# A graph layer's edge loop: weights, edge attributes and index offsets read from SBUF instead of PSUM, one-hot tiles built per twelve tiles

## The chip, the core and the metric

The kernel runs on one core of a Trainium2 chip. The metric is the device time of one execution in microseconds. The engines are TensorE (PE in the profile), VectorE (DVE), ScalarE (ACT), GpSimd (POOL) and SyncE (SP, which here only starts transfers).

## The reference

A message-passing layer with 12,500 nodes of 160 features (64 scalars, and 32 vectors of 3) and 400,000 edges sorted by destination, all in float32:

```python
h = relu(layernorm(x))
s0, s1 = x0 @ W_sc0 * a, einsum(x1, W_sc1) * a          # self part; x0, x1: scalars, vectors of h
y0, y1 = x0 @ W_l1_0 * a, einsum(x1, W_l1_1) * a        # what is sent; a = node_vec1
w = silu(e16 @ fc_W1) @ fc_W2                             # per edge, 192 weights: a (64), b (64), c (32), d (32)
ys0, ys1 = y0[src], y1[src]                             # gather
e0, e1 = e4[:, :1], e4[:, 1:]                           # 4 numbers per edge
mid0 = concat(w_a * ys0 * e0, w_d * sum_c(ys1 * e1))    # 96 scalars
mid1 = concat((w_b * ys0) x e1, (w_c * e0) x ys1)       # 96 vectors of 3
z0, z1 = zeros.at[dst].add(mid0), zeros.at[dst].add(mid1)
out = x + C_S * s + C_X * (z0 @ W_l2_0, einsum(z1, W_l2_1)) * a
```

Constant factors (fan-in, the number of neighbours) are left out above. In the program `e16` is the (400000, 16) array from which the 192 weights come, and `e4` the (400000, 4) array of `e0` and `e1`.

## The kernel before

**Node stage.** 98 tiles of 128 nodes, two at a time: VectorE makes mean, variance and relu(x - mean), PE turns and multiplies, ScalarE scales rows out of PSUM, one DMA per eight tiles stores the sent rows in the DRAM tensor `y_d`, and GpSimd adds the self part to x in `acc`, which stays in SBUF for the whole kernel.

**Index work.** `relate` (L119 to L159) turns the destination of each edge into `drel`, its distance from the first node of its window; a window is three tiles of 128 edges (`WT`), whose destinations must lie within 32 nodes (`WN`). Edges that lie farther go through a fallback at the end (from L572), a loop that runs zero or one time by a flag. The work runs on VectorE over all 3125 tiles at once, with operands in SBUF.

**Edge loop.** 3125 tiles of 128 edges are handled in blocks of four tiles (`GT`), 782 blocks; three blocks are a group of twelve tiles (`TG`). For a block b:

- `load(b)`: GpSimd gathers 128 rows of `y_d` by the indices in `src_sb` for each tile, one indirect DMA per tile (L398), into a `yg` buffer for the block. There are ten such buffers and the calls run eight blocks ahead (`AHEAD`).
- `hidden_pair`: PE (L407) and ScalarE (L412, silu) make the hidden layer for two blocks each.
- `weigh(b)`: PE writes the 192 weights per edge to the PSUM tile `pw` (L429), of which there are two. `scale` (L349, ScalarE) multiplies the first 96 by `e0` in place, and L350 copies `e1` and `drel` (four numbers per tile) into `pw` behind the weights. These come from `ev`, which `e4_load` and `e4_join` make once per 96 tiles (a DMA to `raw`, then copies of `raw` and `drel` by ScalarE, L445 and L446).
- `select(b)`: VectorE compares `iota` with the `drel` in `pw` (L460), which gives a one-hot tile over 32 nodes, and multiplies it by the three numbers of `e1` in `pw` (L462), into a quarter of `sel`.
- `products(b)`, through `multiply`: VectorE makes `tmp` from `yg` and `e1` (L355), sums it over the three components (L357), and writes the products of weights and rows into `pr` (L358, L359, L360, L362).
- `sums(b)`: PE multiplies `sel` and `pr` (L480), adding over a window's three tiles in PSUM; ScalarE copies a finished window out (L485, L487).
- `turn`, `linear`, `add`, `accumulate`: one group behind, one stage per block (`accumulate` in the third): transposes, the output weights, a 0/1 matrix `place` (L508) that puts the windows' rows onto two node tiles, and two additions into `acc` by VectorE (L525).

The order on PE, ScalarE and VectorE is the order of the calls, written out by hand (`manual_schedule`); GpSimd and SP run their own instructions in program order as semaphores allow. For block b the loop calls `load(b + 8)`, `weigh(b + 2)`, a stage of the group before, `select(b + 1)`, `products(b + 1)`, perhaps `accumulate`, `sums(b)`, and on every fourth block `hidden_pair`. At the end `acc` goes to the output in twelve large DMAs.

Of the kernel before, what the change touches and what calls it, by code (L numbers as in the profile page):

```python
# [10 lines left out]
F32 = mybir.dt.float32  # L11
I32 = mybir.dt.int32
AF = mybir.ActivationFunctionType
ALU = mybir.AluOpType
# [4 lines left out]
P = 128  # L19
M0 = 64  # L20
M1 = 32
# [3 lines left out]
NW = 2 * M0 + 2 * M1  # L25
PC = 256
ZC = 384
GT = 4
BT = 32
WN = 32  # L30
WT = 3
GW = 4
TG = WT * GW
EG = 8
# [8 lines left out]
def kernel(  # L43
# [19 lines left out]
    nc = tc.nc  # L63
    N = x.shape[0]
    NT = attr.shape[1]
    TP = src.shape[1]
    T = n_edges // P
    assert n_edges % P == 0 and TP % BT == 0 and NT == (N + P - 1) // P and NT >= 2
    NWIN = (T + WT - 1) // WT
    NG = (NWIN + GW - 1) // GW  # L70
# [11 lines left out]
    iota = const.tile([P, 2 * P], F32, name="iota")  # L82
# [14 lines left out]
    drel = const.tile([P, TP], F32, name="drel")  # L97
# [135 lines left out]
    with (  # L233
# [83 lines left out]
        with tc.manual_schedule(engines=engines):  # L317
# [8 lines left out]
            for q in range(len(steps) + 4):  # L326
                if q <= last and steps[q][2] == 0:
                    g = steps[q][0] + LEAD * GN
# [14 lines left out]
    before.close()  # L343


    def scale(pw, ev, n):

        for k in range(n):
            nc.scalar.activation(pw[:, k, 0:96], pw[:, k, 0:96], AF.Copy, scale=ev[:, k, 0:1])  # L349
        nc.scalar.activation(pw[:, :n, NW:NW + 4], ev[:, :n, 1:5], AF.Copy)  # L350

    def multiply(pr, tmp, wt, yg, n):

        y1 = yg[:, :n, M0:].rearrange("p t (c u) -> p t c u", c=3)
        nc.vector.tensor_tensor(tmp[:, :n, 0:3, :], y1, wt[:, :n, NW:NW + 3].unsqueeze(3).to_broadcast([P, n, 3, M1]),  # L355
                                ALU.mult)
        nc.vector.tensor_reduce(tmp[:, :n, 3, :], tmp[:, :n, 0:3, :].rearrange("p t c u -> p t u c"), AX.X, ALU.add)  # L357
        nc.vector.tensor_mul(pr[:, :n, 192:PC], wt[:, :n, 96:160], yg[:, :n, 0:M0])  # L358
        nc.vector.tensor_mul(pr[:, :n, 0:M0], wt[:, :n, 0:M0], yg[:, :n, 0:M0])  # L359
        nc.vector.tensor_mul(pr[:, :n, 96:192].rearrange("p t (c u) -> p t c u", c=3),  # L360
                             wt[:, :n, M0:96].unsqueeze(2).to_broadcast([P, n, 3, M1]), y1)
        nc.vector.tensor_mul(pr[:, :n, M0:96], wt[:, :n, 160:NW], tmp[:, :n, 3, :])  # L362

    with (
        tc.tile_pool(name="selp", bufs=3) as selp,
        tc.tile_pool(name="prod", bufs=3) as prod,
        tc.tile_pool(name="ld", bufs=2) as ld,
        tc.tile_pool(name="ev", bufs=2) as evp,
        tc.tile_pool(name="yg", bufs=10) as ygp,
        tc.tile_pool(name="hid", bufs=4) as hid,  # L370
        tc.tile_pool(name="post", bufs=2) as post,
# [4 lines left out]
        blocks, ev4, hids, rows, wts, sels, z_ps, z_sb, zT, o_sb, prs, sums_ps = ({} for _ in range(12))  # L376

        def tiles_of(b):
            return list(range(b * GT, min((b + 1) * GT, T)))
# [41 lines left out]
        def weigh(b):  # L421
            hT = hids[b // 2]
            pw = p_w.tile([P, GT, 256], F32, name="pw")
            n = len(tiles_of(b))
            for k in (0, 2, 1, 3):
                if k < n:
                    r = slice(FC_H * (k // 2), FC_H * (k // 2 + 1))
                    o = P * (b % 2 * 2 + k % 2)
                    nc.tensor.matmul(pw[:, k, 0:NW], hT[r, o:o + P], w2[r, :], start=True, stop=True)  # L429
            scale(pw, e4_of(b), n)  # L430
            wts[b] = pw

        def e4_load(q):

            if q * EG < NG and q not in ev4:
                lo, hi = q * EG * TG, min((q + 1) * EG * TG, TP)
                raw = ld.tile([P, EG * TG, 4], F32, name="raw")
                nc.sync.dma_start(raw[:, :hi - lo, :].rearrange("p t c -> p (t c)"), e4[:, lo * 4:hi * 4])
                ev = evp.tile([P, EG * TG, 5], F32, name="ev")
                ev4[q] = ev, raw, lo, hi - lo  # L440

        def e4_join(q):
            if q in ev4:
                ev, raw, lo, n = ev4[q]
                nc.scalar.activation(ev[:, :n, 0:4], raw[:, :n, :], AF.Copy)  # L445
                nc.scalar.activation(ev[:, :n, 4:5], drel[:, lo:lo + n].unsqueeze(2), AF.Copy)  # L446

        def e4_of(b):
            g, k = divmod(b, TG // GT)
            o = g % EG * TG + k * GT  # L450
            return ev4[g // EG][0][:, o:o + GT, :]

        def select(b):

            g, k = divmod(b, TG // GT)
            if k == 0:
                sels[g] = selp.tile([P, TG, 4, WN], F32, name="sel")
            n, wt = len(tiles_of(b)), wts[b]
            sel = sels[g][:, k * GT:k * GT + n, :, :]
            nc.vector.tensor_tensor(sel[:, :, 3, :], iota[:, 0:WN].unsqueeze(1).to_broadcast([P, n, WN]),  # L460
                                    wt[:, :n, NW + 3:NW + 4].to_broadcast([P, n, WN]), ALU.is_equal)
            nc.vector.tensor_tensor(sel[:, :, 0:3, :], sel[:, :, 3:4, :].to_broadcast([P, n, 3, WN]),  # L462
                                    wt[:, :n, NW:NW + 3].unsqueeze(3).to_broadcast([P, n, 3, WN]), ALU.mult)

        def products(b):
            wt, yg = wts.pop(b), rows.pop(b)
            pr = prod.tile([P, GT, PC], F32, name="pr")
            tmp = prod.tile([P, GT, 4, M1], F32, name="tmp")
            multiply(pr, tmp, wt, yg, len(tiles_of(b)))
            prs[b] = pr  # L470

        def sums(b):
# [46 lines left out]
        def accumulate(g):  # L519
            ps = sums_ps.pop(g)  # L520
            i = nc.values_load(tile_i[0:1, g:g + 1], engines=[mybir.EngineType.DVE], min_val=0, max_val=NT - 2,
                               skip_runtime_bounds_check_because="clamped to NT - 2 on the chip, and not negative")
            for h in range(2):
                to = acc[:, ds(i + h, 1), :]
                nc.vector.scalar_tensor_tensor(to, ps[:, h:h + 1, :], a_sb[:, ds(i + h, 1)], to,  # L525
                                               op0=ALU.mult, op1=ALU.add)
# [3 lines left out]
        K = TG // GT  # L530
        order = tc.manual_schedule(engines={mybir.EngineType.PE, mybir.EngineType.Activation, mybir.EngineType.DVE})
        with order:
            for b in range(min(AHEAD, NB)):
                load(b)
            e4_load(0)
            e4_join(0)
            hidden_pair(0)
            weigh(0)
            if NB > 1:
                weigh(1)  # L540
            select(0)
            products(0)
            for b in range(NB):
                g, k = divmod(b, K)
                if b + AHEAD < NB:
                    load(b + AHEAD)
                q, r = divmod(b, EG * K)
                if r == 0:
                    e4_load(q + 1)
                if r == EG * K - 4:  # L550
                    e4_join(q + 1)
                if b + 2 < NB:
                    weigh(b + 2)
                if g:
                    (turn, linear, add)[k](g - 1)
                if b + 1 < NB:
                    select(b + 1)
                    products(b + 1)
                if g and k == K - 1:
                    accumulate(g - 1)  # L560
                sums(b)
                if b % 4 == 0 and b + 4 < NB:
                    hidden_pair((b + 4) // 2)
            for h in ([NG - 2] if NG > 1 else []) + [NG - 1]:
                for k, stage in enumerate((turn, linear, add, accumulate)):
                    if h == NG - 1 or min(k, K - 1) > (NB - 1) % K:
                        stage(h)
# [4 lines left out]
    with (  # L572
# [10 lines left out]
        n = nc.values_load(far_i[0:1, 0:1], min_val=0, max_val=1)  # L583
        with tc.For_i(0, n, 1) as _:
            with tc.For_i(0, ZR, P) as r:
                nc.sync.dma_start(z_d[ds(r, P), :], zero)
            with tc.For_i(0, TP // GT, 1) as g:
                xe = fp.tile([FC_IN, 512], F32, name="f_xe")
                nc.sync.dma_start(xe, e16[ds(g * FC_IN, FC_IN), :])
                er = fp.tile([P, GT, 4], F32, name="f_er")  # L590
                nc.sync.dma_start(er.rearrange("p t c -> p (t c)"), e4[:, ds(g * (GT * 4), GT * 4)])
                ev = fp.tile([P, GT, 5], F32, name="f_ev")
                nc.vector.memset(ev, 0.0)
                si = fp.tile([P, GT], I32, name="f_si")
                nc.sync.dma_start(si, src[:, ds(g * GT, GT)])
                di = fp.tile([P, GT], I32, name="f_di")
# [2 lines left out]
                nc.vector.tensor_copy(df, di)  # L599
                out_of = fp.tile([P, GT], F32, name="f_out")  # L600
                nc.vector.tensor_scalar(out_of, drel[:, ds(g * GT, GT)], float(WN), None, ALU.is_ge)
                nc.vector.tensor_mul(ev[:, :, 0:4], er, out_of.unsqueeze(2).to_broadcast([P, GT, 4]))
                yg = fp.tile([P, GT, D], F32, name="f_yg")
                for k in range(GT):
                    nc.gpsimd.indirect_dma_start(
# [6 lines left out]
                pw = fpw.tile([P, GT, 256], F32, name="f_pw")  # L612
# [1 line left out]
                    nc.tensor.matmul(pw[:, k, 0:NW], hT[:, P * k:P * (k + 1)], w2[0:FC_H, :],  # L614
                                     start=True, stop=True)
                tmp = fp.tile([P, GT, 4, M1], F32, name="f_tmp")
                scale(pw, ev, GT)
                pr = fp.tile([P, GT, PC], F32, name="f_pr")
                multiply(pr, tmp, pw, yg, GT)
                for k in range(GT):  # L620
                    pd = fpp.tile([P, P], F32, name="f_pd")
                    nc.tensor.transpose(pd, df[:, k:k + 1].to_broadcast([P, P]), ident)
                    sel = fp.tile([P, P], F32, name="f_sel")
# [83 lines left out]
```

## Time and profile before

| what | value |
|---|---|
| median of 3 runs | 4176.25 us (4176.24 to 4178.38) |
| the profiled execution | 4178.38 us, its span 4176.5 us |
| POOL busy | 3003.1 us (72%), of which gathers L398 2962.3 us, 3125 of 948 ns |
| PE busy | 3326.4 us (80%), L480 1592.0, L429 758.8 |
| DVE busy | 2885.1 us (69%), six lines of `multiply` 2187, L460 and L462 649 |
| ACT busy | 2641.8 us (63%), L349 985.4, L487 667.5 |
| DMA | 319.85 MB, 77 GB/s over the span |
| gathers | first starts at 219.8 us, last at 4132.8 us |

A share of busy time is over the whole span. A group's row gives an instruction's line, engine, operation, tiles and count, then its busy time, the mean duration of one in ns, and the time that the engine was idle just before it with what ended most of that. Matmuls are pipelined, so a busy PE isn't one at its peak. In rows of the timeline the first two numbers are start and duration in microseconds from the span's start. The names `pw` and `wt` mean one tile in the kernel before: functions that take `wt` are given the PSUM tile `pw`.

### The profile page before, as it was taken

How to read it: one execution, taken by the hardware profiler on the slowest of the kernel's cores; microseconds unless marked ns; L12 is line 12 of the kernel's file. 1: busy time of each engine (PE TensorE's matmuls, PEld its weight loads, DVE VectorE, ACT ScalarE, POOL GpSimd, SP SyncE). 2: the span in 40 equal slices, each digit the busy share in tenths (PEclk: the TensorE clock that was granted, in tenths of full speed). 3: DMA queues.
4: the chain of work that ended last, by engine and by line, in shares of the span. 5: the costliest groups of instructions: out<-in, count | busy, mean ns of one | idle time of the engine just before them, and what ended most of it. 6: DMA issues, size and time to landing. Idle time of an engine off the chain costs nothing.

```text
span 4176.5 us, 61508 instructions
## 1 busy us (share of the span) xinstructions
PE 3326.4 (80%) x17265; PEld 2401.9 (58%) x17265; DVE 2885.1 (69%) x7403; ACT 2641.8 (63%) x9266; POOL 3003.1 (72%) x3150
## 2 busy tenths in 40 slices
PE   8968788877788887788777878777877877778885
PEld 5645555555556555555555555555655555555554
DVE  5477776777777777777777777777777777777774
ACT  3356666666666666666666666666666666666664
POOL 1177777777777777777777777777777777777774
PEclk9999999999999999999999999999999999999998
DMA  4222222222222222222222222222222222222224
GB/s 122 59 78 76 74 76 77 73 76 71 76 76 74 76 76 74 74 74 76 76 73 76 73 76 74 74 76 74 76 76 73 76 74 74 76 74 75 74 72 117
DMA packets 233168, 319.85 MB, mean 77 GB/s; under 512 B 65754, under 2 KB 182566, under 8 KB 232566
## 3 DMA queue, kind: packets, MB, share of 16 engines
q0 software_dynamic: 150000, 256.20, 23.0%
q1 hardware_dynamic: 63412, 47.69, 3.9%
q10 hardware_dynamic: 19410, 11.99, 1.0%
q8 instruction: 139, 2.28, 0.2%
q14 instruction: 207, 1.70, 0.1%
HBM read 299.62 MB, written 16.00 MB: 76 GB/s over the span
## 4 chain that ended last, share of the span: by engine, by line
DVE 24%; DMA 23%; POOL 22%; issue 20%; PE 9%; DVEq 1%; ACT 1%; POOLq 0%
DMA yg<-y_d,src_sb 23%; POOL yg L398 22%; DVE tmp L357 5%; DVE tmp L355 5%; DVE pr L360 3%; DVE pr L359 3%; PE po L299 2%; DVE sel L462 2%; DVE acc L525 2%; DVE pr L362 2%; PE po L298 2%; PE pz L480 1%; DVE sel L460 1%; DVE pr L358 1%; PE pw L429 1%
## 5 line engine op out<-in xcount | busy, mean ns | idle before, releaser
L398 POOL DMA_INDIRECT yg<-y_d,src_sb x3125 | 2962.3, 948 | 953.3 <-issue 736.1
L480 PE MATMUL pz<-pr,sel 128*128 128x256 f32 x6250 | 1592.0, 401 | 0.0
L349 ACT ACTIVATE pw<-pw,ev 128x96 f32<-128x96 f32 x3125 | 985.4, 315 | 938.3 <-PE pw L429 844.4
L429 PE MATMUL pw<-w,hT 64*128 64x192 f32 x6250 | 758.8, 363 | 714.3 <-DVE pr L362 708.1
L480 PEld LDWEIGHTS pz<-pr,sel 128*128 128x128 f32 x6250 | 1228.8, 205 | 151.2 <-issue 0.9
L429 PEld LDWEIGHTS pw<-w,hT 64*128 64x128 f32 x6250 | 515.2, 194 | 1107.6 <-DVE pr L362 956.7
L355 DVE TENSOR_TENSOR tmp<-yg,pw 128x384 f32<-128x384 f32 x782 | 432.7, 553 | 1041.2 <-DMA yg<-y_d,src_sb 1040.3
L487 ACT ACTIVATE zs<-pz 32x64 f32<-32x64 f32 x3126 | 667.5, 214 | 41.4
L357 DVE TENSOR_REDUCE tmp<-tmp 128x128 f32<-128x384 f32 x782 | 463.5, 593 | 27.0
L462 DVE TENSOR_TENSOR sel<-sel,pw 128x384 f32<-128x384 f32 x782 | 432.8, 553 | 26.9
L485 ACT ACTIVATE zs<-pz 32x192 f32<-32x192 f32 x1042 | 337.0, 323 | 152.9 <-PE pz L480 122.8
L360 DVE TENSOR_TENSOR pr<-pw,yg 128x384 f32<-128x384 f32 x782 | 427.1, 546 | 0.0
L407 PE MATMUL px<-xe,w 32*128 32x512 f32 x782 | 294.1, 650 | 69.7 <-issue 58.3
L412 ACT ACTIVATE hT<-px 128x512 f32<-128x512 f32 x391 | 218.4, 595 | 166.6 <-PE px L407 158.4
L358 DVE TENSOR_TENSOR pr<-pw,yg 128x256 f32<-128x256 f32 x782 | 323.4, 414 | 0.0
L359 DVE TENSOR_TENSOR pr<-pw,yg 128x256 f32<-128x256 f32 x782 | 322.7, 413 | 0.0
L504 PE MATMUL px<-wo,za 128*128 128x160 f32 x1566 | 308.7, 338 | 0.4 <-ACT za L497 0.4
L504 PEld LDWEIGHTS px<-wo,za 128*128 128x128 f32 x1566 | 240.0, 204 | 62.3 <-issue 45.7
L460 DVE TENSOR_TENSOR sel<-iota,pw 128x128 f32<-128x128 f32 x782 | 216.4, 277 | 34.6 <-ACT pw L350 34.2
L516 PE MATMUL px<-os,place 128*128 128x160 f32 x1044 | 220.2, 335 | 0.4 <-ACT os L506 0.4
L362 DVE TENSOR_TENSOR pr<-pw,tmp 128x128 f32<-128x128 f32 x782 | 218.0, 279 | 0.0
L525 DVE SCALAR_TENSOR_TENSOR acc<-px,a_sb,acc 128x160 f32 x522 | 197.6, 378 | 11.4 <-PE px L516 2.2
(81 smaller groups left out, 1621.1 us busy)
## 6 DMA issues: line engine op xcount, KB each, us to landing
yg<-y_d,src_sb POOLq DMA_INDIRECT x3125
xe<-in_e SPq DMA_DIRECT2D x784, 32.0 KB
xt<-in_x SPq DMA_DIRECT2D x12, 640.0 KB
y_d<-ys ACTq DMA_DIRECT2D x12, 640.0 KB
raw<-in_e SPq DMA_DIRECT2D x32, 192.0 KB
out<-acc SPq DMA_DIRECT2D x6, 640.0 KB
out<-acc ACTq DMA_DIRECT2D x6, 640.0 KB
dst_i<-in_dst SPq DMA_DIRECT2D x1, 1568.0 KB
```

The source lines that it names most:

```text
L349: nc.scalar.activation(pw[:, k, 0:96], pw[:, k, 0:96], AF.Copy, scale=ev[:, k, 0:1])
L355: nc.vector.tensor_tensor(tmp[:, :n, 0:3, :], y1, wt[:, :n, NW:NW + 3].unsqueeze(3).to_broadcast([P, n, 3, M1]), ALU.mult)
L357: nc.vector.tensor_reduce(tmp[:, :n, 3, :], tmp[:, :n, 0:3, :].rearrange("p t c u -> p t u c"), AX.X, ALU.add)
L358: nc.vector.tensor_mul(pr[:, :n, 192:PC], wt[:, :n, 96:160], yg[:, :n, 0:M0])
L359: nc.vector.tensor_mul(pr[:, :n, 0:M0], wt[:, :n, 0:M0], yg[:, :n, 0:M0])
L360: nc.vector.tensor_mul(pr[:, :n, 96:192].rearrange("p t (c u) -> p t c u", c=3), wt[:, :n, M0:96].unsqueeze(2).to_broadcast([P, n, 3, M1]) ...
L398: nc.gpsimd.indirect_dma_start(out=yg[:, k, :], out_offset=None, in_=y_d, in_offset=bass.IndirectOffsetOnAxis(ap=src_sb[:, t:t + 1], axis=0))
L429: nc.tensor.matmul(pw[:, k, 0:NW], hT[r, o:o + P], w2[r, :], start=True, stop=True)
L462: nc.vector.tensor_tensor(sel[:, :, 0:3, :], sel[:, :, 3:4, :].to_broadcast([P, n, 3, WN]), wt[:, :n, NW:NW + 3].unsqueeze(3).to_broadcast ...
L480: nc.tensor.matmul(pz[:, 0:PC], sels[g][:, t % TG, :, :], pr[:, k, :], start=t % WT == 0, stop=last)
L487: nc.scalar.activation(zs[:, 192 + M0 * c:192 + M0 * (c + 1)], pz[WN * c:WN * (c + 1), 192:PC], AF.Copy)
L504: nc.tensor.matmul(po[:m, :], za[:, k, :m], wo[:, k, :], start=k == 0, stop=k == 2)
```

## The change

`scale` writes to a new SBUF tile `wt` (three buffers): the 96 scaled weights of each tile, and one copy of the other 96 for the whole block. The copies of `e1` and `drel` into PSUM are gone. `ev` is now the DMA's own target in SBUF, with four numbers per edge; `e4_group` starts this DMA where a group first asks for it, and `e4_load`, `e4_join` and the tile with five numbers are gone. `multiply` reads `e1` from `ev` and the weights from `wt`. `select` works on a whole group of twelve tiles: one comparison of `iota` with `drel`, four multiplications of three tiles each; it is called once per group, behind `products(b + 1)` of the group's second block, for the next group. The fallback loop follows in the same manner. Node stage, index work, gathers, matmuls and output are as they were.

```diff
--- before.py
+++ after.py
@@ -343,16 +343,16 @@
     before.close()
 
 
-    def scale(pw, ev, n):
+    def scale(wt, pw, ev, n):
 
         for k in range(n):
-            nc.scalar.activation(pw[:, k, 0:96], pw[:, k, 0:96], AF.Copy, scale=ev[:, k, 0:1])
-        nc.scalar.activation(pw[:, :n, NW:NW + 4], ev[:, :n, 1:5], AF.Copy)
-
-    def multiply(pr, tmp, wt, yg, n):
+            nc.scalar.activation(wt[:, k, 0:96], pw[:, k, 0:96], AF.Copy, scale=ev[:, k, 0:1])
+        nc.scalar.activation(wt[:, :n, 96:NW], pw[:, :n, 96:NW], AF.Copy)
+
+    def multiply(pr, tmp, wt, yg, ev, n):
 
         y1 = yg[:, :n, M0:].rearrange("p t (c u) -> p t c u", c=3)
-        nc.vector.tensor_tensor(tmp[:, :n, 0:3, :], y1, wt[:, :n, NW:NW + 3].unsqueeze(3).to_broadcast([P, n, 3, M1]),
+        nc.vector.tensor_tensor(tmp[:, :n, 0:3, :], y1, ev[:, :n, 1:4].unsqueeze(3).to_broadcast([P, n, 3, M1]),
                                 ALU.mult)
         nc.vector.tensor_reduce(tmp[:, :n, 3, :], tmp[:, :n, 0:3, :].rearrange("p t c u -> p t u c"), AX.X, ALU.add)
         nc.vector.tensor_mul(pr[:, :n, 192:PC], wt[:, :n, 96:160], yg[:, :n, 0:M0])
@@ -365,7 +365,6 @@
         tc.tile_pool(name="selp", bufs=3) as selp,
         tc.tile_pool(name="prod", bufs=3) as prod,
         tc.tile_pool(name="ld", bufs=2) as ld,
-        tc.tile_pool(name="ev", bufs=2) as evp,
         tc.tile_pool(name="yg", bufs=10) as ygp,
         tc.tile_pool(name="hid", bufs=4) as hid,
         tc.tile_pool(name="post", bufs=2) as post,
@@ -427,46 +426,41 @@
                     r = slice(FC_H * (k // 2), FC_H * (k // 2 + 1))
                     o = P * (b % 2 * 2 + k % 2)
                     nc.tensor.matmul(pw[:, k, 0:NW], hT[r, o:o + P], w2[r, :], start=True, stop=True)
-            scale(pw, e4_of(b), n)
-            wts[b] = pw
-
-        def e4_load(q):
-
-            if q * EG < NG and q not in ev4:
-                lo, hi = q * EG * TG, min((q + 1) * EG * TG, TP)
-                raw = ld.tile([P, EG * TG, 4], F32, name="raw")
-                nc.sync.dma_start(raw[:, :hi - lo, :].rearrange("p t c -> p (t c)"), e4[:, lo * 4:hi * 4])
-                ev = evp.tile([P, EG * TG, 5], F32, name="ev")
-                ev4[q] = ev, raw, lo, hi - lo
-
-        def e4_join(q):
-            if q in ev4:
-                ev, raw, lo, n = ev4[q]
-                nc.scalar.activation(ev[:, :n, 0:4], raw[:, :n, :], AF.Copy)
-                nc.scalar.activation(ev[:, :n, 4:5], drel[:, lo:lo + n].unsqueeze(2), AF.Copy)
+            wt = prod.tile([P, GT, NW], F32, name="wt")
+            scale(wt, pw, e4_of(b), n)
+            wts[b] = wt
+
+        def e4_group(g):
+            if g // EG not in ev4:
+                lo, hi = g // EG * EG * TG, min((g // EG + 1) * EG * TG, TP)
+                ev = ld.tile([P, EG * TG, 4], F32, name="ev")
+                nc.sync.dma_start(ev[:, :hi - lo, :].rearrange("p t c -> p (t c)"), e4[:, lo * 4:hi * 4])
+                ev4[g // EG] = ev
+            return ev4[g // EG][:, g % EG * TG:(g % EG + 1) * TG, :]
 
         def e4_of(b):
             g, k = divmod(b, TG // GT)
-            o = g % EG * TG + k * GT
-            return ev4[g // EG][0][:, o:o + GT, :]
-
-        def select(b):
-
-            g, k = divmod(b, TG // GT)
-            if k == 0:
-                sels[g] = selp.tile([P, TG, 4, WN], F32, name="sel")
-            n, wt = len(tiles_of(b)), wts[b]
-            sel = sels[g][:, k * GT:k * GT + n, :, :]
-            nc.vector.tensor_tensor(sel[:, :, 3, :], iota[:, 0:WN].unsqueeze(1).to_broadcast([P, n, WN]),
-                                    wt[:, :n, NW + 3:NW + 4].to_broadcast([P, n, WN]), ALU.is_equal)
-            nc.vector.tensor_tensor(sel[:, :, 0:3, :], sel[:, :, 3:4, :].to_broadcast([P, n, 3, WN]),
-                                    wt[:, :n, NW:NW + 3].unsqueeze(3).to_broadcast([P, n, 3, WN]), ALU.mult)
+            return e4_group(g)[:, k * GT:(k + 1) * GT, :]
+
+        def select(g):
+
+            ev = e4_group(g)
+            lo, hi = g * TG, min((g + 1) * TG, T)
+            n = hi - lo
+            sel = selp.tile([P, TG, 4, WN], F32, name="sel")
+            nc.vector.tensor_tensor(sel[:, :n, 3, :], iota[:, 0:WN].unsqueeze(1).to_broadcast([P, n, WN]),
+                                    drel[:, lo:hi].unsqueeze(2).to_broadcast([P, n, WN]), ALU.is_equal)
+            for t in range(0, n, WT):
+                m = min(WT, n - t)
+                nc.vector.tensor_tensor(sel[:, t:t + m, 0:3, :], sel[:, t:t + m, 3:4, :].to_broadcast([P, m, 3, WN]),
+                                        ev[:, t:t + m, 1:4].unsqueeze(3).to_broadcast([P, m, 3, WN]), ALU.mult)
+            sels[g] = sel
 
         def products(b):
             wt, yg = wts.pop(b), rows.pop(b)
             pr = prod.tile([P, GT, PC], F32, name="pr")
             tmp = prod.tile([P, GT, 4, M1], F32, name="tmp")
-            multiply(pr, tmp, wt, yg, len(tiles_of(b)))
+            multiply(pr, tmp, wt, yg, e4_of(b), len(tiles_of(b)))
             prs[b] = pr
 
         def sums(b):
@@ -532,32 +526,26 @@
         with order:
             for b in range(min(AHEAD, NB)):
                 load(b)
-            e4_load(0)
-            e4_join(0)
+            select(0)
             hidden_pair(0)
             weigh(0)
             if NB > 1:
                 weigh(1)
-            select(0)
             products(0)
             for b in range(NB):
                 g, k = divmod(b, K)
                 if b + AHEAD < NB:
                     load(b + AHEAD)
-                q, r = divmod(b, EG * K)
-                if r == 0:
-                    e4_load(q + 1)
-                if r == EG * K - 4:
-                    e4_join(q + 1)
                 if b + 2 < NB:
                     weigh(b + 2)
                 if g:
                     (turn, linear, add)[k](g - 1)
                 if b + 1 < NB:
-                    select(b + 1)
                     products(b + 1)
                 if g and k == K - 1:
                     accumulate(g - 1)
+                if k == 1 and g + 1 < NG:
+                    select(g + 1)
                 sums(b)
                 if b % 4 == 0 and b + 4 < NB:
                     hidden_pair((b + 4) // 2)
...
```

More of the change, by code (lines that the diff above doesn't have):

```diff
@@ L589 @@
                 nc.sync.dma_start(xe, e16[ds(g * FC_IN, FC_IN), :])
[L590 to L593, printed above, removed]
+                ev = fp.tile([P, GT, 4], F32, name="f_ev")
+                nc.sync.dma_start(ev.rearrange("p t c -> p (t c)"), e4[:, ds(g * (GT * 4), GT * 4)])
                 si = fp.tile([P, GT], I32, name="f_si")
@@ L601 @@
                 nc.vector.tensor_scalar(out_of, drel[:, ds(g * GT, GT)], float(WN), None, ALU.is_ge)
-                nc.vector.tensor_mul(ev[:, :, 0:4], er, out_of.unsqueeze(2).to_broadcast([P, GT, 4]))
+                nc.vector.tensor_mul(ev, ev, out_of.unsqueeze(2).to_broadcast([P, GT, 4]))
                 yg = fp.tile([P, GT, D], F32, name="f_yg")
@@ L616 @@
                 tmp = fp.tile([P, GT, 4, M1], F32, name="f_tmp")
-                scale(pw, ev, GT)
+                wt = fp.tile([P, GT, NW], F32, name="f_wt")
+                scale(wt, pw, ev, GT)
                 pr = fp.tile([P, GT, PC], F32, name="f_pr")
-                multiply(pr, tmp, pw, yg, GT)
+                multiply(pr, tmp, wt, yg, ev, GT)
                 for k in range(GT):
```

## The prediction

> **What bounds the kernel now.** I read the page first: its busy line, then its costliest groups.
>
> ```profile
> PE 3326.4 (80%) x17265; PEld 2401.9 (58%) x17265; DVE 2885.1 (69%) x7403; ACT 2641.8 (63%) x9266; POOL 3003.1 (72%) x3150
> L398 POOL DMA_INDIRECT yg<-y_d,src_sb x3125 | 2962.3, 948 | 953.3 <-issue 736.1 <-DVE sel L462 102.4 <-DVE sel L460 72.2
> ```
>
> PE has the largest share, but the groups point to POOL: the idle time before its 3125 gathers is 953.3 us, or 0.305 us each, always the same and mostly put down to "issue". The table of windows confirms it:
>
> ```profile
> 400.00:800.00 400.00, 323.30 (x1707) 233.23 (x1706) 282.94 (x721) 261.59 (x927) 302.50 (x320) 0.94 0.28 75
> ```
>
> The fifth busy column is POOL: 320 gathers in 400 us, one every 1.250 us (0.946 busy, 0.305 to the next). A block of four tiles takes 4 x 1.25 = 5.0 us whatever the others do. The view of waits agrees: VectorE's longest wait is for the gathered rows, and PE's for VectorE; both follow POOL.
>
> ```profile
> DVE tmp L355 <- DMA yg<-y_d,src_sb: 1040.3, 735, 3.6
> PEld pw L429 <- DVE pr L362: 956.7, 539, 3.9
> ```
>
> The tile view of `yg` has the first gather at 219.8 us and the last at 4132.8. The time is so 219.8 us of node stage, 3913 us of gathers at 1.250 (with the longer first ones below), and 43.7 us of tail. The edge loop's engines can only move the result by moving the 1.250 us.
>
> Then the timeline where gathers and index work overlap, before the edge loop starts (start, duration, engine, line):
>
> ```profile
> 226.68 0.70 DVE L144 TENSOR_SCALAR lim<-lim 128x1044 f32<-128x1044 f32 x1
> 227.14 1.06 POOL L398 DMA_INDIRECT yg<-y_d,src_sb  x1 [0.30 <-issue]
> 227.30 3.40 DVE L150 TENSOR_TENSOR drel<-drel,negb 128x3123 f32<-128x3123 f32 x1
> 228.50 3.01 POOL L398 DMA_INDIRECT yg<-y_d,src_sb  x1 [0.30 <-issue]
> 230.74 3.41 DVE L151 TENSOR_TENSOR over<-drel,lim 128x3123 f32<-128x3123 f32 x1
> 231.82 3.15 POOL L398 DMA_INDIRECT yg<-y_d,src_sb  x1 [0.30 <-issue]
> 234.07 0.15 DVE L150 TENSOR_TENSOR drel<-drel,negb 128x2 f32<-128x2 f32 x1
> 234.45 3.41 DVE L153 TENSOR_REDUCE far<-over 128x1 f32<-128x3125 f32 x1
> 235.27 0.95 POOL L398 DMA_INDIRECT yg<-y_d,src_sb  x1 [0.30 <-issue]
> 237.77 0.95 POOL L398 DMA_INDIRECT yg<-y_d,src_sb  x1 [0.30 <-issue]
> 237.78 3.44 DVE L155 SCALAR_TENSOR_TENSOR drel<-over,drel 128x3125 f32<-128x3125 f32 x1
> 239.02 3.01 POOL L398 DMA_INDIRECT yg<-y_d,src_sb  x1 [0.30 <-issue]
> ```
>
> A gather that starts while VectorE runs an operation with two SBUF inputs (L150, L151, L155) is held until about 0.13 us before that operation's end, and then takes its 0.946: 227.30 + 3.40 - 0.13 + 0.946 = 231.52, and the gather of 228.50 ends at 231.51. L153, one input, delays nothing (0.95). The gather of 237.77, 0.01 us ahead of L155, isn't delayed either: only the gather's start needs what VectorE holds. The gather of 231.82 gets in at the end of L151 although the two-input L150 of 234.07 follows at once.
>
> In the edge loop every two-input operation of VectorE has one input in PSUM now (`pw`), and the gathers stay at 0.95. The one exception is L508 (`place`), SBUF alone: by the trace, gathers that start 17 to 54 ns after it began take 0.946, those 146 to 193 ns after take 1.010 to 0.967, as here:
>
> ```profile
> 2192.40 0.34 DVE L508 TENSOR_SCALAR place<-iota,at 128x256 f32<-128x256 f32 x1
> 2192.57 0.98 POOL L398 DMA_INDIRECT yg<-y_d,src_sb  x1 [0.30 <-DVE pr L362]
> ```
>
> So an operation can hold up a gather that starts in a window from about 0.10 us (between 0.054 and 0.146) after its start to 0.13 us before its end.
>
> **The change part by part.** *Inputs to SBUF.* `wt`, `ev`, `drel` and `iota` are all in SBUF afterwards, so L355, L358, L359, L360, L362, the comparison and the multiplications of `select` all have two SBUF inputs. The number of elements stays, and L150 (3123 elements in 3.40) and L358 (256 in 0.41, one input in PSUM) lie on one line, 1.04 ns per element and 0.15 fixed, so VectorE itself is not slower. What is new is the windows. If gathers met them at random, the delay per gather would be half the sum of the squared windows over the 5.0 us of a block. Windows (duration less 0.23): L355 and L360 0.32 each, L358 and L359 0.18 each, L362 0.05; per three blocks one comparison of 384 elements (0.32) and four products of 288 (0.45 by the line, window 0.22). Squares: 0.205 + 0.065 + 0.003 + 0.034 + 0.065 = 0.372; half of it over 5.0 is 0.037 us, times 3125 = 116 us. With the opening at 0.054 or 0.146 instead of 0.10 it is 163 or 79.
>
> But they don't meet at random: L355 waits for the last gather of its block, so both run in step. In this block
>
> ```profile
> 2003.99 0.56 DVE L355 TENSOR_TENSOR tmp<-yg,pw 128x384 f32<-128x384 f32 x1 [1.75 <-DMA yg<-y_d,src_sb]
> 2005.08 0.41 DVE L358 TENSOR_TENSOR pr<-pw,yg 128x256 f32<-128x256 f32 x1
> 2006.21 0.28 DVE L362 TENSOR_TENSOR pr<-pw,tmp 128x128 f32<-128x128 f32 x1
> ```
>
> gathers start at 2003.83, 2005.08, 2006.33 and 2007.58. The first misses L355 by starting ahead of it; the second starts with L358 and misses; the third is in L362's window (2006.31 to 2006.36): 0.03 us. The fourth, in one block of three, meets the new `select`: comparison from 2006.41, products from 2007.00 every 0.36, so it is in the second product's window (2007.46 to 2007.68): 0.10 us. That pushes the next block's gathers back by 0.13 against its L355, and the one that missed L358 is then in its window: 0.15. Per three blocks 3 x 0.03 + 0.10 + 0.15 = 0.34 us, or 0.113 per block, times 781 blocks = 88 us. I take this, since it is read from the phase that the loop has; the random sum (79 to 163) keeps the upper end. Below, nothing excludes that jitter lets nearly all gathers miss: 0.
>
> The Trainium skill (SBUF — State Buffer, "Who interferes with whom") says that a VectorE instruction with two SBUF inputs contends with a GpSimd instruction that reads SBUF, but that a probe's `tensor_tensor` did not stall DMA, from which it infers that descriptor generation needs the write side alone. By that remark this part would cost nothing, and the time would be 4175 us; the 3.01 us gather beside L150 here speaks against it, so I go by the row.
>
> *Select once per twelve tiles.* Before, per three blocks, 3 x (277 + 554) = 2493 ns of L460 and L462; after, 554 + 4 x 449 = 2350. VectorE loses 0.14 us per three blocks, 37 us in all, off the path. It moves from the wait ahead of L355 to behind the products, in one block of three: 2.5 us of products, 2.1 of `select`, 0.34 of L508 fill 4.9 of 5.0 us. A lateness of some tenths is caught up in the next two blocks; POOL would notice only when a `yg` buffer (ten blocks) is not free.
>
> *ScalarE.* Four scalings 315 ns and L350 187 ns per block, 1.45 us, become four of 96 elements into SBUF (214 ns for 64, 288 for 160: about 245) and one copy of 4 x 96 (L497's form, 486): 1.47. The joins L445 and L446 (28.7 us in all) go. Net nothing; ScalarE is busy 3.2 of 5.0 us, and that idle time covers it.
>
> *PE and PSUM.* `pw` is free after ScalarE's copy instead of after L362, so the 956.7 us wait of L429 goes; PE then waits at L480 for `pr`, which L362 of the same block still ends. Gain only in the tail, where L429's 0.84 us lay in the chain behind L362: -1 us.
>
> *Queues.* On SP the `e4` load (33 of 192 KB) stays and is asked for at first use; its buffer's last user ended 24 blocks earlier, so SP issues it ahead, between `xe` loads. Without that cover 3.4 us each (issued 244.94, L445 at 248.34), 112 us on VectorE, most of it absorbed by the ten buffers. On POOL nothing is added or moved.
>
> Sum: the profiled execution took 4178.4 us (span 4176.5 and 1.9 around it), 2.1 over the median of 4176.25; 4178.4 + 88 - 1 = 4265, against the median 4263.
>
> **The rivals.** (a) *The gathers slip through: not slower.* L355 starts at a fixed distance behind the last gather's landing, so the phase may settle where every gather starts ahead of a window, as three of the four above do. For: the second gather misses L358 by its opening alone. Against: `select` fills 2.1 us of one block in three, longer than a gather's pitch. It decides if the mean delay stays under 0.0027 us per gather; time 4176.25 - 1 = 4175. (b) *A held gather does not get in between two operations.* L358 to L362 follow one another without a gap (1.4 us), and `select` runs for 2.1 us. With windows of 0.32, 1.2 and, in one block of three, 1.9 us, half the squares are 1.4 per block; over a block of 6.0 us that is 0.24 us per gather, +740 us, so 4900; with the phase kept perhaps 4700. For: the operations overlap by 0.08 us in the trace. Against: the gather of 231.82, which got in ahead of the L150 of 234.07, though that one has 2 elements only. (c) *VectorE loses instead*, waiting for the gather's reading. L155 beside a fresh gather took 3.44 where L151 took 3.41: 0.03 us for each of four gathers is well inside the 1.3 us that L355 waits per block (1040.3 / 782); no cost.
>
> **How the numbers follow.** Held gathers at 14 to 224 us more: 0.77, likeliest 4263, its own range 4190 to 4400. (a) with (c): 0.13, of which 0.02 ends faster by the tail. (b): 0.10. The range 4180 to 4430 leaves out most of (a) and (b). A measurement of this kernel tells apart about 0.2%, 8.4 us: faster 0.02, same 0.11, slower 0.87.
>
> **What would show it.** Right: L398's mean rises from 948 to about 975 ns, the 0.305 between gathers stays, and lengthened gathers end 0.82 us after L358, L362 or a product of `select` ends; the wait of L429 for L362 is gone and the time isn't. Gathers all at 0.946 are (a); gathers of 1.5 us and more in the loop are (b). Wrong in kind would be POOL idle beyond 0.305 us, or a VectorE that no longer waits for `yg`.

## The result, and the profile after

The changed kernel takes 4332.79 us (median of 4 runs, 4331.9 to 4333.49), the kernel before 4176.24. The ratio is 1.0373, 95% interval 1.0356 to 1.0391: slower by 156.5 us. The forecast was 4263 (87 us slower), in a range of 4180 to 4430.

The page of the changed kernel: its busy line, and from the costliest groups the gathers and L355.

```profile
PE 3517.8 (81%) x17265; PEld 2446.1 (56%) x17265; DVE 2851.3 (66%) x7142; ACT 2549.6 (59%) x9200; POOL 3158.7 (73%) x3150
L397 POOL DMA_INDIRECT yg<-y_d,src_sb x3125 | 3117.8, 998 | 953.4 <-issue 891.6
L355 DVE TENSOR_TENSOR tmp<-yg,ev 128x384 f32<-128x384 f32 x782 | 436.2, 558 | 1281.2 <-DMA yg<-y_d,src_sb 1277.2
```

(Gathers are L397 now; the lines of `multiply` keep their numbers; the comparison of `select` is L451, its products L455, `place` L502, `accumulate` L519.) The gathers' busy time is 3117.8 us where it was 2962.3: 155.5 us more, the whole difference: the spans of the two profiled executions differ by 153.6 us, as the tail behind the last gather is 2.0 us shorter. The idle time ahead of the gathers is the same to 0.1 us. VectorE waits longer for rows than before, and is busy for less: it didn't become the bound; the gathers themselves got longer. The window from 400 to 800 us has 308 gathers where there were 320, one every 1.30 us:

```profile
400.00:800.00 400.00, 328.25 (x1635) 227.88 (x1634) 269.30 (x669) 241.03 (x880) 306.40 (x308) 0.91 0.27 72
```

The median gather still takes 946 ns. The mean is higher because some 1100 of them are long. The timeline shows what they are long by; first the gathers, then VectorE's operations:

```profile
2004.06 1.03 POOL L397 DMA_INDIRECT yg<-y_d,src_sb  x1 [0.30 <-issue]
2009.14 1.06 POOL L397 DMA_INDIRECT yg<-y_d,src_sb  x1 [0.30 <-issue]
2010.51 1.02 POOL L397 DMA_INDIRECT yg<-y_d,src_sb  x1 [0.30 <-issue]
2013.09 0.94 POOL L397 DMA_INDIRECT yg<-y_d,src_sb  x1 [0.30 <-issue]
2014.33 1.04 POOL L397 DMA_INDIRECT yg<-y_d,src_sb  x1 [0.30 <-issue]
```

```profile
2003.99 0.28 DVE L362 TENSOR_TENSOR pr<-wt,tmp 128x128 f32<-128x128 f32 x1
2009.10 0.28 DVE L362 TENSOR_TENSOR pr<-wt,tmp 128x128 f32<-128x128 f32 x1
2009.88 1.56 DVE L455 TENSOR_TENSOR sel<-sel,ev 128x288 f32<-128x288 f32 x4
2013.08 0.46 DVE L358 TENSOR_TENSOR pr<-wt,yg 128x256 f32<-128x256 f32 x1
2014.27 0.28 DVE L362 TENSOR_TENSOR pr<-wt,tmp 128x128 f32<-128x128 f32 x1
```

The gather of 2004.06 starts 0.07 us into L362, which ends at 2004.27; the gather ends at 2005.09, 0.82 us later. So do those of 2009.14 (L362 ends at 2009.38) and 2014.33 (L362 ends at 2014.55). The one of 2010.51 starts in the second of the four products, which ends at about 2010.69, 0.82 us ahead of the gather's end. The one of 2013.09 starts 0.01 us after L358 and isn't held; L358 takes 0.46 instead of its usual 0.41.

Sorted by this sign (a gather more than 8 ns over 946 is put down to the VectorE operation that ends 0.82 us ahead of its end), the holds in the edge loop are, in us:

| operation | changed kernel | weights in PSUM | weights alone in SBUF | 0.1 us later | 0.5 us later |
|---|---|---|---|---|---|
| L355 | 23.7 | 13.9 | 0 | 25.3 | 6.4 |
| L358 | 35.1 | 0 | 20.4 | 14.7 | 4.3 |
| L359 | 3.8 | 0 | 1.5 | 4.3 | 2.3 |
| L360 | 15.4 | 0 | 17.1 | 15.6 | 160.1 |
| L362 | 36.3 | 0 | 47.3 | 40.5 | 0.6 |
| comparison of `select` | 7.6 | 2.3 | 0 | 2.2 | 0 |
| products of `select` | 31.5 | 30.9 | 0 | 43.5 | 69.7 |
| all gathers' time over 946 ns, less that under it | 152.6 | 45.4 | 85.2 | 145.1 | 242.3 |

The columns are runs told of below, with the operations under the changed kernel's lines.

### The profile page after: what moved, and what is told of

Read it like the earlier page. It is cut to its first block, busy times and chain, and to the rows that moved or that the text cites. A ratio compares the mean times of both kernels' runs of the same rounds, so it can differ in the third digit from the quotient of the medians.

```text
span 4330.1 us, 61825 instructions
## 1 busy us (share of the span) xinstructions
PE 3517.8 (81%) x17265; PEld 2446.1 (56%) x17265; DVE 2851.3 (66%) x7142; ACT 2549.6 (59%) x9200; POOL 3158.7 (73%) x3150
## 4 chain that ended last, share of the span: by engine, by line
POOL 45%; issue 31%; DMA 12%; PE 6%; DVE 5%; DVEq 0%; ACT 0%; POOLq 0%; ACTq 0%
POOL yg L397 45%; DMA yg<-y_d,src_sb 11%; PE po L299 2%; PE po L298 2%; DVE tmp L355 1%; PE pz L474 1%; DVE pr L358 1%; DVE acc L519 1%; DVE pr L360 1%; DVE pr L362 1%; DVE pr L359 0%; PE pt L282 0%; PE pt L283 0%; PE pw L428 0%; DVE sel L455 0%
## 5 line engine op out<-in xcount | busy, mean ns | idle before, releaser
L397 POOL DMA_INDIRECT yg<-y_d,src_sb x3125 | 3117.8, 998 | 953.4 <-issue 891.6
L474 PE MATMUL pz<-pr,sel 128*128 128x256 f32 x6250 | 1680.5, 416 | 586.3 <-DVE pr L362 584.7
L474 PEld LDWEIGHTS pz<-pr,sel 128*128 128x128 f32 x6250 | 1235.4, 207 | 843.5 <-DVE pr L362 445.8
L355 DVE TENSOR_TENSOR tmp<-yg,ev 128x384 f32<-128x384 f32 x782 | 436.2, 558 | 1281.2 <-DMA yg<-y_d,src_sb 1277.2
L349 ACT ACTIVATE wt<-pw,ev 128x96 f32<-128x96 f32 x3125 | 808.2, 344 | 340.4 <-ACT zs L481 217.2
L360 DVE TENSOR_TENSOR pr<-wt,yg 128x384 f32<-128x384 f32 x782 | 428.5, 548 | 0.0
L455 DVE TENSOR_TENSOR sel<-sel,ev 128x288 f32<-128x288 f32 x1042 | 407.7, 453 | 8.9
L350 ACT ACTIVATE wt<-pw 128x384 f32<-128x384 f32 x782 | 398.8, 510 | 0.0
L358 DVE TENSOR_TENSOR pr<-wt,yg 128x256 f32<-128x256 f32 x782 | 334.1, 427 | 0.1
L359 DVE TENSOR_TENSOR pr<-wt,yg 128x256 f32<-128x256 f32 x782 | 324.5, 415 | 0.0
L406 PEld LDWEIGHTS px<-xe,w 32*128 32x128 f32 x782 | 86.8, 199 | 291.1 <-issue 275.1
L362 DVE TENSOR_TENSOR pr<-wt,tmp 128x128 f32<-128x128 f32 x782 | 219.7, 281 | 0.0
```

Source lines behind the costliest of these rows:

```text
L349: nc.scalar.activation(wt[:, k, 0:96], pw[:, k, 0:96], AF.Copy, scale=ev[:, k, 0:1])
L350: nc.scalar.activation(wt[:, :n, 96:NW], pw[:, :n, 96:NW], AF.Copy)
L355: nc.vector.tensor_tensor(tmp[:, :n, 0:3, :], y1, ev[:, :n, 1:4].unsqueeze(3).to_broadcast([P, n, 3, M1]), ALU.mult)
L397: nc.gpsimd.indirect_dma_start(out=yg[:, k, :], out_offset=None, in_=y_d, in_offset=bass.IndirectOffsetOnAxis(ap=src_sb[:, t:t + 1], axis=0))
L406: nc.tensor.matmul(ph, w1[r, :], xe[r, :], start=True, stop=True)
L455: nc.vector.tensor_tensor(sel[:, t:t + m, 0:3, :], sel[:, t:t + m, 3:4, :].to_broadcast([P, m, 3, WN]), ev[:, t:t + m, 1:4].unsqueeze(3).t ...
```

## The experiments

Theories: that a two-input operation on SBUF holds up gathers (the port theory of the expectations); that the time comes from `select` making VectorE late; and, within the first, whether the phase between gathers and VectorE counts or only the share of time held. Ratios are to the kernel before, run beside each experiment; there it took between 4177 and 4186 us (and 5915 in one case told of below), so ratios and differences are compared, not times.

**Weights back in PSUM.** The changed kernel, with one input of L358 to L362 in PSUM again:

```diff
             nc.scalar.activation(wt[:, k, 0:96], pw[:, k, 0:96], AF.Copy, scale=ev[:, k, 0:1])
-        nc.scalar.activation(wt[:, :n, 96:NW], pw[:, :n, 96:NW], AF.Copy)
...
-            wt = prod.tile([P, GT, NW], F32, name="wt")
-            scale(wt, pw, e4_of(b), n)
-            wts[b] = wt
+            scale(pw, pw, e4_of(b), n)
+            wts[b] = pw
```

> The changed kernel, but the weights are scaled in place and read from PSUM by L358 to L362, as in the kernel before; e1 (L355) and select keep two SBUF inputs. Port theory (a gather whose start falls into a VectorE operation with two SBUF inputs, from about 0.02 us after its start to 0.13 us before its end, is held until then, and the sum of these holds is the whole difference): what remains are the holds by L355 and select, 30 to 65 us, so 4205 to 4240, the gathers' mean at 956 to 967 ns, and no gather that ends 0.82 us after L358 to L362. Rival, random meeting (the share of time locked counts, not the phase): 103 of 200 us by the squared windows, 4279. Rival, lateness (select once per twelve tiles makes VectorE late, the port has no part in it): unchanged at 4333.

Measured: 4243.85 us, ratio 1.0141 (1.0124 to 1.0158), 58.9 us over its kernel before. No gather is held by L358 to L362, and 45.4 us of holds by L355 and `select` are left, within the 30 to 65 and far from the 103 of random meeting. The rest isn't in the loop, so that the time lies near the expected one is partly luck. The first gather starts at 242.0 us instead of 219.8, behind the index work:

```profile
242.03 1.30 POOL L396 DMA_INDIRECT yg<-y_d,src_sb  x1 [23.92 <-DVE sel L449]
L396 POOL DMA_INDIRECT yg<-y_d,src_sb x3125 | 3002.4, 961 | 975.6 <-issue 883.5
```

That is 22 us later, but the first gathers are no longer held, which gives 7 us back. Why the first gather waits is not shown; perhaps the buffers of the gathered rows came to lie in memory that the index work uses. Lateness falls: `select` runs here as in the changed kernel, and of 153 us of holds 45 are left.

**The weights alone in SBUF.** The complement: the kernel before, with `wt` written by ScalarE and read by L358 to L362, while `e1` and `drel` stay in PSUM:

```diff
-            nc.scalar.activation(pw[:, k, 0:96], pw[:, k, 0:96], AF.Copy, scale=ev[:, k, 0:1])
+            nc.scalar.activation(wt[:, k, 0:96], pw[:, k, 0:96], AF.Copy, scale=ev[:, k, 0:1])
+        nc.scalar.activation(wt[:, :n, 96:NW], pw[:, :n, 96:NW], AF.Copy)
         nc.scalar.activation(pw[:, :n, NW:NW + 4], ev[:, :n, 1:5], AF.Copy)
...
-            scale(pw, e4_of(b), n)
-            wts[b] = pw
+            wt = prod.tile([P, GT, NW], F32, name="wt")
+            scale(wt, pw, e4_of(b), n)
+            wts[b] = wt, pw
```

> The kernel before, but ScalarE writes the weights to an SBUF tile as in the changed kernel, and L358 to L362 read them there; e1 and drel stay in PSUM for L355 and a select per block. Port theory: the holds by L358, L359, L360 and L362 alone, 80 to 125 us, so 4256 to 4301; gathers' mean 972 to 986 ns. Random meeting: 98 us, 4274 (not told apart here). Lateness: 4176, as select is per block again.

Measured: 4274.42 us, ratio 1.0214 (1.0197 to 1.0231), 89.5 us over its kernel before; gathers' mean 976 ns, holds 85.2 us.

```profile
L399 POOL DMA_INDIRECT yg<-y_d,src_sb x3125 | 3049.6, 976 | 953.3 <-issue 739.1
```

The two halves of the change hold 45 and 85 us, 130 together, against 153 in one kernel: presumably each half's holds also move the gathers among the other's operations, but this was not tried by itself.

**One more operation, from SBUF or from PSUM.** Twins of the kernel before, which differ in one operand of an operation whose result nothing uses:

```diff
                     select(b + 1)
+                    extra(b + 1)     # ex <- iota x iota, or ex <- iota x pw; 4 x 192 elements
                     products(b + 1)
```

> The kernel before with one more operation per block that nothing uses: a product of 4 x 192 elements, both inputs in SBUF, between select and products, in VectorE's wait for the gathered rows (0.95 us). Port theory, with the phase of the kernel before: some 470 gathers held by 0.3 us each, 140 us, 4300 to 4330. Random meeting: window 0.80, 0.064 us per gather, 200 us, 4376. If VectorE's time were what counts: the same time as with the PSUM input of the twin run.

> The twin of the run with one more operation: the same product of 4 x 192 elements at the same place, but the second input is the weights in PSUM. Port theory and random meeting: nothing held, 4176 to 4178, gathers' mean 948. If VectorE's time counts: like the twin.

Measured: with SBUF 4394.15 us, ratio 1.0504 (1.0486 to 1.0521); with PSUM 4185.06, ratio 0.9999 (0.999 to 1.0009). The groups of the two kernels by form, the SBUF one first:

```profile
L398 POOL DMA_INDIRECT yg<-y_d,src_sb x3125 | 3172.9, 1015 | 953.3 <-issue 804.7 <-DVE sel L460 47.2 <-DVE ex L468 41.7
L468 DVE TENSOR_TENSOR ex<-iota 128x768 f32<-128x768 f32 x780 | 742.9, 952 | 0.0
```

```profile
L398 POOL DMA_INDIRECT yg<-y_d,src_sb x3125 | 2970.2, 950 | 954.0 <-issue 822.3 <-DVE sel L460 68.3 <-DMA yg<-y_d,src_sb 23.2
L468 DVE TENSOR_TENSOR ex<-iota,pw 128x768 f32<-128x768 f32 x780 | 738.3, 947 | 0.0
```

The operation costs VectorE the same 0.95 us in both, and 209 us or nothing in time; the gathers' busy time differs by 203 us, their idle time by under 1. So neither VectorE's load nor the number of operations counts, but that both inputs are in SBUF. The size was missed: 407 gathers are held by 0.51 us each, where 470 by 0.30 were expected from the phase; random meeting said 200 and came closer here.

**VectorE 0.1 and 0.5 us later.** The changed kernel, with a one-input operation ahead of L355 that moves the phase and holds nothing:

```diff
+            n = len(tiles_of(b))
+            late = prod.tile([P, GT], F32, name="late")
+            nc.vector.tensor_reduce(late[:, :n], yg[:, :n, 0:8], AX.X, ALU.add)      # the other run: 0:104
             multiply(pr, tmp, wt, yg, e4_of(b), len(tiles_of(b)))
```

> The changed kernel with a reduction of 4 x 8 elements of the gathered rows (one input, result unused) ahead of L355, which puts VectorE's sequence about 0.1 us later against the gathers and locks nothing. Port theory with phase: L358 starts after the gather that it held, so its holds fall and L362's grow; a walk through the sequence with the durations of the trace gives 105 to 115 us of holds against 127 to 170 for the changed kernel as it is, so 15 to 50 us below it, 4285 to 4320. Random meeting: unchanged, 4333 within 5. Lateness: 4333 or a little more.

> The same with 4 x 104 elements: VectorE's sequence about 0.5 us later. Port theory with phase: the third gather of a block now starts in L360, some 700 times by 0.25 us; 240 us of holds, 4405 to 4435. Random meeting: unchanged, 4333 within 5. Lateness: half a microsecond per block of VectorE time, which its 1.3 us of waiting hides: 4333.

Measured: 0.1 us later 4328.49 us, ratio 1.0364 (1.0348 to 1.038), which can't be told from the changed kernel's 1.0373: a miss. The table shows that L358's holds fell by 20 us and L362's grew by 4 as expected, but those of `select`'s products grew by 12 too. 0.5 us later: 4421.17 us, ratio 1.0581 (1.0565 to 1.0597), 244.5 us over before, as the walk through the phase said (240), now nearly all by L360 and `select`. From its timeline, VectorE and then a gather:

```profile
2006.91 0.58 DVE L465 TENSOR_REDUCE late<-yg 128x4 f32<-128x416 f32 x1 [1.58 <-DMA yg<-y_d,src_sb]
2009.17 0.56 DVE L360 TENSOR_TENSOR pr<-wt,yg 128x384 f32<-128x384 f32 x1
```

```profile
2009.29 1.26 POOL L397 DMA_INDIRECT yg<-y_d,src_sb  x1 [0.30 <-issue]
```

The third gather of a block starts 0.12 us into L360 and is held for 0.31. The idle time between gathers stays at 0.305 us in both runs, so lateness has no part in it. The two-input operations of VectorE are the same in all three kernels; their phase against the gathers makes 145, 153 or 242 us of holds, so random meeting, which gives one loss for all three, falls as a rule for a given phase.

**The index work away from the first gathers.** The same holds cost the kernel before 7.6 us at its first gathers. The first try gives the index work memory of its own:

```diff
+    rp = before.enter_context(tc.tile_pool(name="rel", bufs=1))
...
-    with tc.tile_pool(name="rel", bufs=1) as rp, tc.tile_pool(name="rel_p", bufs=1, space=PSUM) as rpp:
+    with tc.tile_pool(name="rel_p", bufs=1, space=PSUM) as rpp:
```

> The kernel before with the index work's tiles given memory of their own ahead of the node stage, so that relate (two SBUF inputs over 3123 elements) starts when VectorE is through with the node tiles, at about 203 us, and no longer waits until 219 for the memory. Port theory: L150 and L151 lie ahead of the first gather, one hold of up to 2.1 us by L155 is left of the 7.6 us that the first gathers were long by; 4168 to 4172. Rival, the first gathers are long by themselves (first use): 4176 still.

Measured: 4182.25 us, ratio 1.0013 (1.0004 to 1.0022): slower by 5.6 us. No longer bound by memory, the index work was placed at 60 to 89 us, among the node tiles, where PE waits 11.1 us for it (1.5, 5.9 and 3.6 us); the first gather starts at 232.7 instead of 219.8. The holds are gone as expected: the first gather takes 1.30 us, the next 0.95.

```profile
232.73 1.30 POOL L399 DMA_INDIRECT yg<-y_d,src_sb  x1 [2.45 <-DMA xe<-in_e]
234.33 0.95 POOL L399 DMA_INDIRECT yg<-y_d,src_sb  x1 [0.30 <-issue]
```

So the second try puts it behind the last node tile by order:

```diff
+                if q == last + 1:
+                    far = relate(rp)
```

> The kernel before with the index work in memory of its own and called at the end of the node stage's own order, behind the last scales, so that VectorE does it in its wait from 203 to 225 us and not among the node tiles; the count of far edges (a matmul and a minimum) stays behind. Port theory: L150 and L151 end ahead of the first gather at about 220, which then meets L155 alone; of the 7.6 us by which the first gathers were long 2.1 to 2.5 stay, so 5 us less than before, 4171 (ratio 0.9988). Rival, something else than the port makes the first gathers long: 4176. If VectorE's work here delays the node stage as in the run before: over 4180.

Beside this run the kernel before took 5915.22 us, this one 5911.3 (ratio 0.9996, 0.9969 to 1.0024), with PE at a granted clock of 0.78 instead of some 0.94. POOL was no longer the bound (0.84 us from one gather to the next, not 0.305), so the time tells nothing of the gathers. It was run again:

> The index work in one piece behind the last node tile, once more, beside a kernel before that takes its usual 4180 or so. The trace of the first run shows the last addition of GpSimd held by L151 (first gather 2.2 us later) and one gather held by 2.4 us by L155, of 7.6 us before: 3 us less than before, ratio 0.9993.

Measured: 4182.98 us, ratio 0.9994 (0.9985 to 1.0003), 3.0 us less, as expected, though not beyond the interval. In the timeline VectorE and GpSimd hold each other, in both directions (VectorE's rows first):

```profile
214.84 5.98 DVE L152 TENSOR_TENSOR over<-drel,lim 128x3123 f32<-128x3123 f32 x1
225.11 3.40 DVE L156 SCALAR_TENSOR_TENSOR drel<-over,drel 128x3125 f32<-128x3125 f32 x1
```

```profile
213.80 7.74 POOL L317 TENSOR_TENSOR acc<-ys,xt 128x1280 f32<-128x1280 f32 x2 [12.96 <-ACT ys L314]
225.97 3.37 POOL L405 DMA_INDIRECT yg<-y_d,src_sb  x1 [0.30 <-issue]
```

L152 takes 5.98 us instead of 3.41 beside GpSimd's two additions, which take 7.74 instead of 2.88 + 0.86; then L156 holds a gather until 0.13 us before its end. The third version cuts the work into six pieces, each ahead of VectorE's 8 us wait for a square root:

```diff
+                if q > 12 and q <= last and steps[q - 1][2] + steps[q - 1][3] == steps[q - 1][1]:
+                    next(pieces, None)
```

> The kernel before with the index work cut into pieces (at most 9 us each), one ahead of each wait of 8 us that VectorE has for the square root at the end of a group of node tiles, in memory of its own. Port theory: no operation with two SBUF inputs over 3123 elements is left beside a gather, so all first gathers take 0.95 to 1.30 us, and as the waits cover the pieces the first gather still starts at about 220: 7 us less than before, 4169 where before takes 4176 (ratio 0.9983). Rival, the first gathers are long by themselves: no change. If a piece delays the node tiles, the first gather starts later by as much.

Measured: 4180.23 us where before takes 4185.97, ratio 0.9987 (0.9978 to 0.9996): 5.7 us less than the kernel before, and the lowest ratio of all runs.

```profile
221.21 1.30 POOL L413 DMA_INDIRECT yg<-y_d,src_sb  x1 [2.23 <-DMA xe<-in_e]
222.81 0.96 POOL L413 DMA_INDIRECT yg<-y_d,src_sb  x1 [0.30 <-issue]
224.08 0.95 POOL L413 DMA_INDIRECT yg<-y_d,src_sb  x1 [0.30 <-issue]
```

All gathers are short; the first starts 1.4 us later than before, which takes that much of the 7 expected.

## Why the prediction was right, and where its sum was short

- **The bound.** Right: POOL's gathers set the time, before and after, and what moved it was their duration. From the first gather's start to the last's it is 3913.1 us before and 4068.7 after.
- **The mechanism.** Right, and shown by the twins: both inputs in SBUF cost 209 us, one in PSUM nothing. The sign of a held gather, an end 0.82 us after the operation's, holds for all lines.
- **The size of the windows** is the term that was mis-sized. The prediction put their opening at about 0.10 us after an operation's start, between 0.054 and 0.146, from L508, an operation with one SBUF tensor. For those with two the trace of after shows it near the start itself: of the gathers that start in L358, 109 of 121 are free up to 0.03 us in and 149 of 150 are held from there on; in L355 they are held from 0.05 us on, in L362 from 0.01 on. Of the 154 us of holds in the loop, 96 are of gathers that start less than 0.10 us into the operation, which the prediction's windows let through. Random meeting with windows of an operation's duration less 0.15 us, over blocks of 5.2 us, would be about 196 us, not 116; that is above what was measured.
- **The phase of one block, taken for all.** The three terms of the sum measured L362 36 us (23 forecast), the products of `select` 31 (26), L358 35 (39): 103 against 88. That they come so near is partly luck: all 401 gathers held by L362 and 125 of the 161 held by L358 start less than 0.10 us in. Left out were the operations that the gathers of the shown block miss: L355 23.7, L360 15.4, the comparison 7.6, L359 3.8, together 50.5 us. The trace of before has blocks where they don't: by an estimate from the starts of all its gathers, with windows from 0.03 us behind an operation's start to 0.13 ahead of its end, L360 would hold 88 of them for 12 us, L355 37 for 8 and L359 17 for 3. The rest presumably comes from the holds, each of which pushes the following gathers along VectorE's sequence; that was not shown by itself.
- **The other edits.** VectorE's busy time fell by 34 us (37 forecast), ScalarE's by 92 (nothing net forecast), both off the path. One scaling into SBUF was put at about 245 ns, where the line through the two rows named there gives 239; measured are 259 (808.2 us over 3125). L429's wait for L362 is gone, and PE waits for L362 at the sums instead (584.7 us, now L474). The tail behind the last gather's start is 41.7 us instead of 43.7 (1 us less was forecast).
- **The rivals.** (a), slipping through, falls: 1100 of 3125 gathers are held. (b), a gather held through a run of operations, falls: they end 0.82 us after one operation's end while the next has begun. (c) is there but small: L358 takes 440 ns on average where a gather starts at most 0.06 us ahead of it or 0.04 behind its start, and 414 otherwise. Under (a) the prediction counts three of four gathers as ahead of a window, though by its own reading the third lies in L362's.

The Trainium skill (SBUF — State Buffer, "Who interferes with whom") was weighed on the remark that a `tensor_tensor` did not stall DMA. The twins decide against it for gathers whose indices lie in SBUF: 209 us from such an operation. The same page ("SBUF: two separate sides") says that whichever engine starts first keeps the shared pair of ports for the whole instruction. GpSimd's additions beside L152 (7.74 and 5.98 us) agree with it; a gather doesn't, since L155 started 0.01 us behind one (237.77 and 237.78 in the prediction's timeline) and took 3.44 us, where a wait for the whole gather would have made it over 4.3.

## What to carry to other kernels

Where GpSimd issues the transfers that set the time, look where VectorE's inputs lie before counting its microseconds: with its second input in PSUM the added operation was free, and with both in SBUF each one of 0.95 us cost 0.27 us on average on an engine that it has nothing to do with. When two engines run in step, one block's phase gives the sign and the suspects of such a loss, but not its size (88 us of 153 here). Take the starts of all gathers in the trace of before instead of one block's; the random sum is no upper end, as the run 0.5 us later lost 242 us. A wait of VectorE hides more of its work only if that work doesn't hold up the engine that sets the time.

## What was not expected of the hardware

- A gather is held only at its start: an operation that begins 0.01 us behind it doesn't lengthen it (0.95 us beside L155), nor did one that began 0.01 us ahead (0.94 beside L358). It costs the operation little: the longest L358 of the changed kernel is 486 ns against 414 without a gather at its start.
- GpSimd's two additions (1280 and 320 elements) and VectorE's comparison of 3123 hold each other up: 7.74 us instead of 3.74 for the two, 5.98 instead of 3.41 for the comparison.
- A phase shift of 0.5 us between two engines changed the time by 88 us (ratio 1.0581 against 1.0373) with the same instructions on the bounding engine.
